# Interpolating two chunks with diagonal matmuls, and moving the opening's sums from VectorE to ScalarE and TensorE

## The chip, the core and the metric

The kernel runs on one core of a Trainium2 chip. The engines are TensorE (PE, with its weight loads PEld), VectorE (DVE), ScalarE (ACT), GpSimd (POOL) and SyncE (SP, which here issues most DMAs). Each engine runs its own instructions in order. Matmuls write PSUM, and results have to be copied from there. The metric is device time of one execution in microseconds; before the change it is 7589.68 us, the median of 3 runs (7587.77 to 7598.68).

## What is computed

Two layers over an image of 4 batches x 128 channels x 64 x 64. The first is a deformable convolution: every output position reads nine taps, each at a fractional position that a small convolution predicts, so each tap is a weighted sum of four neighbours ("corners").

```
def deform_forward(x, w_off, b_off, w_mask, b_mask, weight, bias):
    offset = conv2d(x, w_off, b_off)
    mask = jax.nn.sigmoid(conv2d(x, w_mask, b_mask))
...
    samples = bilinear_sample(x, py, px)
    samples = samples * mask[:, None]
...
    out = jnp.einsum('bckhw,ock->bohw', samples, w_flat)
    return out + bias[None, :, None, None]
```

The second is attention of 16 heads of 8 over the 4096 positions of each batch, with queries, keys and values from the same cosine features, then a small feed-forward layer and a choice of two experts of eight:

```
    qkv = _qz_ring(heads + rx_theta)
    q = jnp.transpose(qkv, (0, 2, 1, 3))
    scores = jnp.einsum('bhsd,bhtd->bhst', q, q) / np.sqrt(D)
    attn = jax.nn.softmax(scores, axis=-1)
    ctx = jnp.einsum('bhst,bhtd->bhsd', attn, q)
```

Everything is float32, and all 4096 keys of a batch are attended to by all its queries.

## The kernel before

**Chunks and units.** A batch is cut into 8 chunks of 512 positions. `prepare` brings a batch through normalization, a table of corners in DRAM, the offsets (`offsets`, which gives the gather indices and the corner weights `wt`), and then `deform`, which walks over units: 12 to a chunk, each of 128 positions and 3 taps. For a unit POOL issues three indirect DMAs (L625) that bring, for each position, four corners of 128 channels into `v`. DVE multiplies `v` with the weights (L645, 1536 elements a partition) and adds twice (L650, L651), which leaves three tap samples with positions on the partitions. The convolution needs channels on the partitions.

**Two ways to turn the samples.** In most chunks DVE transposes blocks (L686), a DMA stores them to `smd`, and `convolved` reads them back as `sT`. In the first two chunks of batch 0 TensorE transposes them (three transposes a unit, L662) into PSUM, and DVE copies the result to `sT_first` (L665) one unit later: the copy waits in the list `moved`. After the last unit of a chunk, `convolved` runs 18 matmul steps (nine taps, two halves; L281 is the helper `by_columns`, which makes each product of four column pieces), DVE adds bias and input (L758), and `features` turns the chunk into keys, queries and values, stored to DRAM with SP and loaded by the attention. `offsets` leaves the indices and weights of the image's second half in `rest`; in batch 0 they are computed after the last unit of chunk 0. Gathers run up to four units ahead in the first three chunks.

**Attention as a list of runs.** A run is one query chunk, one group of four heads and some key tiles of 128. Each step (`scores`, two exponentials on ACT of 128x1024, then `context`) handles one tile; the context of a run adds up in a single PSUM bank, `acc`. Scores are issued up to two steps ahead. Batch 0 starts before all its chunks exist, so its first runs take only the keys at hand: run kinds FIRST, MORE and LAST leave partial sums in DRAM (`partd`). FIRST stores its sum. MORE loads the earlier sum into `cu` at its first step (L1454), DVE adds `acc` (L1488) and the sum is stored again (L1126). Here `opening` counts the first 26 runs: 12 FIRST and 14 MORE, with chunk 0 (16 steps), chunk 1 (48), chunk 2 (40) and chunk 3 (56). Every MORE run among them has four steps.

**Order.** PE, DVE, SP and POOL get their order by hand: the class `Beside` plans, step by step, which pieces of the preparation go between attention steps. A piece announces its cost on PE and DVE with `need(pe=..., dve=..., lat=..., after=...)`; `beside.now`, `beside.dve` and `beside.pool` are the planned times, and `beside.later(when, emit)` issues a DMA when the plan reaches that time. At the end of a run the plan sets DVE's time to at least 1.9 us after the present step and adds the sum. ACT alone is ordered by the scheduler. Until chunk 0 is ready (`alone`) PSUM for the preparation comes from the three score tiles, afterwards from one bank, `ps_m`. The tag `st` has three buffers, `v` three, `cu` two, `acc` one.

Of the kernel before, what the change touches and what calls it, by code (L numbers as in the profile page):

```python
# [9 lines left out]
F32 = mybir.dt.float32  # L10
# [214 lines left out]
def kernel(  # L225
# [373 lines left out]
    def deform(b, tab, idx, wt, rest):  # L599
# [12 lines left out]
        def gather(last):  # L612

            nonlocal issued
            while issued < len(units) and issued <= last + (4 if early(issued) else 2):
# [12 lines left out]
                    )  # L628
                ahead.append((v, beside.gathered()))

        sent = 0.0
        moved = []
        gather(-1)
        for n, (ch, kg, j) in enumerate(units):
            progress[b] = 0.1 + 0.9 * n / len(units)
            if b == 0 and n == 36:
                yield need(dve=5.0)
                settle()
            while not ahead:
                yield need(lat=0.5)  # L640
            v, landed = ahead.pop(0)
            v4 = v.rearrange("p k (q c) -> p (k q) c", c=C)
            w12 = wt[:, j, 3 * kg : 3 * kg + 3, :].rearrange("p k q -> p (k q)")
            yield need(dve=ve(1536), after=landed)
            nc.vector.tensor_tensor(v4, v4, w12[:, :, None].to_broadcast([P, 12, C]), ALU.mult)  # L645
            if moved:
                yield need(pe=0.01, dve=ve(384))
                moved.pop()()
            yield need(dve=ve(768) + ve(384))
            nc.vector.tensor_tensor(v[:, :, : 2 * C], v[:, :, : 2 * C], v[:, :, 2 * C :], ALU.add)  # L650
            nc.vector.tensor_tensor(v[:, :, :C], v[:, :, :C], v[:, :, C : 2 * C], ALU.add)  # L651
            if b == 0 and ch < 2:


                if n % 12 == 0:
                    while len(summed) < ch:
                        yield need(lat=0.5)
                    sT = big.tile([P, KK, CH], F32, tag="xs", name=f"sT_first{ch}")
                yield need(pe=tr(3), lat=FREE, hold=True)
                pt = misc(f"sT_ps{j}_{kg}")  # L660
                for k in range(3):
                    nc.tensor.transpose(pt[:, P * k : P * (k + 1)], v[:, k, :C], ident)  # L662

                def move(sT=sT, kg=kg, i=j % 4, pt=pt):
                    nc.vector.tensor_copy(  # L665
                        sT[:, 3 * kg : 3 * kg + 3, P * i : P * (i + 1)],
                        pt[:, : 3 * P].rearrange("p (k c) -> p k c", c=P),
                    )

                moved.append(move)  # L670
                beside.later(beside.now + 0.8, lambda n=n: gather(n))
                if n % 12 == 11:
                    yield need(pe=0.01, dve=ve(384))
                    moved.pop()()
                    featuring.append(True)
                    beside.add("prepare", convolved(b, ch, sT), 0.5, True)
                    if ch == 0:
                        yield from rest
                continue

            yield need(dve=ve(384))
# [36 lines left out]

    def convolved(b, ch, sT=None):
# [16 lines left out]
        if not in_order:  # L736
# [1 line left out]
            yield need(lat=6.0)  # L738
            get(1)
            yield need(lat=4.0)  # L740
        for k in range(KK):
# [378 lines left out]

        beside.later(beside.dve, put)

    def park_sums(g, sc, cu):
# [6 lines left out]
        beside.later(beside.dve, put)  # L1130

# [139 lines left out]
            es.append(e)  # L1271
        return es

    def context(acc, run, t, es):
        b, g, _, ts, _ = runs[run]
        qf = keys[b, g, t // 4][1]
        flat = qf.rearrange("p t x -> p (t x)")
        width = 32 if t == ts[0] else QW
        for h in range(4):
            first = QG * (t % 4) + QW * h  # L1280
            nc.tensor.matmul(  # L1281
                acc[32 * h : 32 * h + width, :],
                lhsT=flat[:, first : first + width],
                rhs=es[h // 2][:, h % 2, :],
                start=(t == ts[0]), stop=(t == ts[-1]),
            )


    WHOLE, FIRST, MORE, LAST = range(4)
# [118 lines left out]
    with tc.manual_schedule(engines={PE, DVE, SP, POOL}):  # L1408
# [6 lines left out]
        while n < len(steps):  # L1415
# [48 lines left out]
            if following:  # L1464
# [7 lines left out]
                if takes[run + 1] and at == len(ts) - 5:  # L1472
                    fetch_values(run + 1)
                    for giver in takes[run + 1]:
                        for kt in range(4):
                            granted(lambda a=(run + 1, giver, kt): fetch(*a))
            context(acc, run, t, es.pop(0))
            n += 1
            if at == 0 and takes[run]:
                beside.add("turned", from_turned(run, acc), -1)  # L1480
            if at < len(ts) - 1:
                continue
            beside.dve = max(beside.dve, beside.now + 1.9) + ve(512)
            if kind in (WHOLE, FIRST):
                cu = work.tile([P, 512], F32, tag="cu", name=f"cu{run}", bufs=NCU)
                nc.vector.tensor_copy(cu, acc)  # L1486
            else:
                nc.vector.tensor_tensor(cu, cu, acc, ALU.add)  # L1488
            if kind in (WHOLE, LAST):
                park_context(b, g, sc, cu)  # L1490
            else:
                park_sums(g, sc, cu)
        alone.append(True)
        beside.drain()

# [72 lines left out]
```

## Time and profile before

| | |
|---|---|
| median of 3 runs | 7589.68 us |
| the profiled execution | 7632.52 us |
| its span, first to last instruction | 7630.7 us |
| PE busy | 7132.4 us (93%) |
| ACT busy | 6855.1 us (90%) |
| DVE busy | 4479.3 us (59%) |
| POOL busy | 1653.8 us (22%) |
| L645 multiply, 128x1536 | 384 x 1735 ns mean |
| L650, L651 adds, 128x768 and 128x384 | 384 x 956 ns, 384 x 562 ns |
| L1486 copy of `acc`, L1488 add | 128 x 691 ns, 38 x 687 ns |
| L1270 exponential, 128x1024 | 7400, 6852.0 us together |

Times in the timeline are microseconds from the start of the span. In a line of the timeline the first number is the start, the second how long it took, and the brackets at the end give how long the engine had been idle and what ended that. In the views of waits the first number is the total in us, the second how often, the third the longest. "Granted clock" is the share of full speed at which TensorE was clocked.

### The profile page before, as it was taken

What the parts mean: (1) busy time and instruction counts of PE and PEld (TensorE: products, weight loads), DVE (VectorE), ACT (ScalarE), POOL (GpSimd) and SP (SyncE); (2) the same over time, 40 slices, a digit from 0 to 9 for tenths busy, and PEclk for the clock granted to TensorE, in tenths of its full rate; (3) what the DMA queues carried; (4) which work ended last, traced back from release to release, by engine and by line L of the source; (5) the groups of instructions that cost most, each with busy time, mean ns of one, the idle gap of its engine ahead of it and who ended that gap; (6) DMA issues with size and microseconds to landing.
All of it is one profiled execution on the core that took longest, in us unless ns stands there. A gap on an engine that the chain in (4) does not pass through costs nothing.

```text
span 7630.7 us, 180510 instructions
## 1 busy us (share of the span) xinstructions
PE 7132.4 (93%) x73736; PEld 2383.1 (31%) x73736; DVE 4479.3 (59%) x8976; ACT 6855.1 (90%) x7441; POOL 1653.8 (22%) x1326
## 2 busy tenths in 40 slices
PE   3679899899999999999999999989999999999997
PEld 2122232223333333333333323323333333333333
DVE  6766356667444867776554677775444545455534
ACT  0569899899999999999999988989999999999995
POOL 5544034443000432422000334331000000000000
PEclk6889999999999999999999999999999999999998
DMA  6677567978445878887655688897554466667662
GB/s 176 208 212 222 137 209 238 302 235 295 151 172 196 289 231 268 282 273 239 203 179 185 232 274 287 286 309 251 184 175 162 148 232 230 234 217 244 222 204 64
DMA packets 909787, 1689.50 MB, mean 221 GB/s; under 512 B 150754, under 2 KB 384124, under 8 KB 858268
## 3 DMA queue, kind: packets, MB, share of 16 engines
q1 hardware_dynamic: 809102, 1371.37, 54.5%
q0 software_dynamic: 92160, 302.06, 12.5%
q8 instruction: 579, 9.49, 0.5%
q10 hardware_dynamic: 7694, 4.52, 0.2%
q14 instruction: 252, 2.06, 0.1%
HBM read 1027.51 MB, written 650.14 MB: 220 GB/s over the span
## 4 chain that ended last, share of the span: by engine, by line
PE 82%; DMA 8%; DVE 4%; issue 3%; ACT 2%; SPq 1%; POOL 1%; another core or an unknown queue 0%; ACTq 0%; POOLq 0%; DVEq 0%
PE acc L1281 40%; PE sc L1261 24%; PE acc L1214 5%; PE e_ps L281 4%; PE conv_ps L281 4%; DMA et<-etd 3%; PE f_ps L281 2%; ACT e L1270 2%; DMA sT<-smd 1%; PE om_ps L533 1%; DMA etd<-st 1%; DVE v L645 1%; DMA smd<-tr 1%; POOL v L625 0%; PE ao_ps L281 0%
## 5 line engine op out<-in xcount | busy, mean ns | idle before, releaser
L1270 ACT ACTIVATE e<-sc 128x1024 f32<-128x1024 f32 x7400 | 6852.0, 1076 | 637.9 <-PE sc L1261 456.3
L1281 PE MATMUL acc<-e,qf 128*9 128x512 f32 (+1 forms) x29600 | 3946.4, 602 | 33.8 <-DVE cu L1488 15.2
L1261 PE MATMUL sc<-qT,kT 32*128 32x512 f32 x14800 | 2380.9, 500 | 193.8 <-ACT e L1270 97.7
L1261 PEld LDWEIGHTS sc<-qT,kT 32*128 32x128 f32 x14800 | 948.2, 183 | 3663.1 <-ACT e L1270 3140.8
L625 POOL DMA_INDIRECT v<-tab,idx x1152 | 1450.7, 1259 | 1679.6 <-DVE tr L686 1058.0
L1140 DVE STREAM_TRANSPOSE st<-e 128x1024 f32<-128x1024 f32 x792 | 937.3, 1221 | 774.8 <-ACT e L1270 651.0
L1281 PEld LDWEIGHTS acc<-e,qf 128*9 128x9 f32 (+1 forms) x29600 | 682.3, 91 | 629.3 <-issue 345.8
L396 POOL TENSOR_TENSOR r<-ln_t,expo 128x4 f32<-128x4 f32 x96 | 112.2, 1170 | 3111.0 <-DVE ln_t L394 3073.8
L645 DVE TENSOR_TENSOR v<-v,wt 128x1536 f32<-128x1536 f32 x384 | 666.1, 1735 | 102.9 <-DMA v<-tab,idx 88.2
L1214 PE MATMUL acc<-et,qv 128*9 128x128 f32 x12672 | 509.2, 277 | 58.9 <-DMA et<-etd 45.5
L1065 DVE TENSOR_TENSOR eo<-e_ps,gt 128x512 f32<-128x512 f32 x256 | 175.2, 686 | 549.1 <-PE e_ps L281 540.3
L650 DVE TENSOR_TENSOR v<-v 128x768 f32<-128x768 f32 x384 | 367.1, 956 | 9.8
L281 PE MATMUL conv_ps<-sT,wconv_sb 128*32 128x256 f32 x4320 | 352.3, 400 | 11.0 <-DMA sT<-smd 8.8
L1214 PEld LDWEIGHTS acc<-et,qv 128*9 128x9 f32 x12672 | 270.8, 90 | 263.2 <-issue 220.9
L1486 DVE COPY cu<-acc 128x512 f32<-128x512 f32 x128 | 88.5, 691 | 349.0 <-PE acc L1281 290.5
L686 DVE STREAM_TRANSPOSE tr<-v 128x128 f32<-128x128 f32 x1080 | 249.3, 281 | 45.2 <-DMA etd<-st 36.5
L651 DVE TENSOR_TENSOR v<-v 128x384 f32<-128x384 f32 x384 | 215.7, 562 | 13.3
L396 POOL TENSOR_TENSOR rstd<-lt_t,expo 128x4 f32<-128x4 f32 x32 | 59.4, 1856 | 515.2 <-DVE lt_t L394 494.9
L281 PE MATMUL f_ps<-w_sb,h 128*32 128x128 f32 x4096 | 167.6, 282 | 1.5 <-issue 1.5
L950 DVE TENSOR_SCALAR h<-h_ps,b_sb 128x512 f32<-128x512 f32 x128 | 94.9, 744 | 100.3 <-PE h_ps L948 85.0
L823 POOL COPY fx<-rn 128x512 f32<-128x512 f32 x32 | 26.9, 840 | 535.2 <-DVE rn L822 338.2
L965 DVE TENSOR_TENSOR a<-a,f_ps 128x512 f32<-128x512 f32 x32 | 22.0, 686 | 202.9 <-PE f_ps L281 202.5
(224 smaller groups left out, 3148.5 us busy)
## 6 DMA issues: line engine op xcount, KB each, us to landing
etd<-st SPq DMA_DIRECT2D x396, 1024.0 KB
et<-etd SPq DMA_DIRECT2D x396, 1024.0 KB
kT<-kTd SPq DMA_DIRECT2D x372, 256.0 KB
smd<-tr SPq DMA_DIRECT2D x360, 192.0 KB
sT<-smd SPq DMA_DIRECT2D x360, 192.0 KB
qT<-qTd SPq DMA_DIRECT2D x166, 256.0 KB
atd<-cu SPq DMA_DIRECT2D x128, 256.0 KB
qf<-fqd SPq DMA_DIRECT2D x372, 72.0 KB
```

Source lines behind the costliest of these rows:

```text
L281: nc.tensor.matmul(dst[c : c + 32], lhsT=lhsT[:, c : c + 32], rhs=rhs, start=start, stop=stop)
L625: nc.gpsimd.indirect_dma_start(out=v[:, k, :], out_offset=None, in_=tab, in_offset=bass.IndirectOffsetOnAxis(ap=idx[:, j, kk : kk + 1], ax ...
L645: nc.vector.tensor_tensor(v4, v4, w12[:, :, None].to_broadcast([P, 12, C]), ALU.mult)
L650: nc.vector.tensor_tensor(v[:, :, : 2 * C], v[:, :, : 2 * C], v[:, :, 2 * C :], ALU.add)
L651: nc.vector.tensor_tensor(v[:, :, :C], v[:, :, :C], v[:, :, C : 2 * C], ALU.add)
L686: nc.vector.transpose(out=tr9[:, k, :, j % 4, :], in_=v[:, k, :C].rearrange("p (c i) -> p c i", i=32),)
L1065: nc.vector.tensor_tensor(ws[hf], pe.rearrange("p (e c) -> p e c", c=C), gt[:, i, 4 * hf : 4 * (hf + 1), None].to_broadcast([P, 4, C]), AL ...
L1140: nc.vector.transpose(out=st[:, :, 2 * pr : 2 * pr + 2, :].rearrange("p o h (q j) -> p o (h q) j", j=32), in_=es[pr].rearrange("p h (q o i ...
L1214: nc.tensor.matmul(acc[32 * h : 32 * h + QW, P * kt : P * (kt + 1)], lhsT=qv[:, at : at + QW], rhs=e[:, :, h, 32 * t : 32 * (t + 1)], star ...
L1261: nc.tensor.matmul(ps[i // 2][:, i % 2, :], lhsT=kT[h : h + 32, P * (t % 4) : P * (t % 4 + 1)], rhs=qT[h : h + 32, :], start=True, stop=True,)
L1270: nc.scalar.activation(e, ps[pr], AF.Exp, scale=1.0 / math.sqrt(HD))
L1281: nc.tensor.matmul(acc[32 * h : 32 * h + width, :], lhsT=flat[:, first : first + width], rhs=es[h // 2][:, h % 2, :], start=(t == ts[0]), ...
```

## The change

The diff has two parts.

*First two chunks of batch 0.* DVE no longer multiplies the gathered corners. It multiplies the identity matrix by the twelve weights of a unit, which gives twelve diagonal matrices of 128 x 128 in `dg` (a buffer of tag `st`). TensorE multiplies each gathered corner block with its diagonal matrix and adds the four corners of a tap in PSUM: product with the weight, sum and transposition are one chain of matmuls. The two DVE adds and the three transposes go. For chunk 0 the convolution's taps are issued as soon as three of its nine are complete in `sT` (function `taps`), into a PSUM tile `po` that is held through the chunk, and `convolved` then skips them. The second half's weights (`rest`) come after unit 5 instead of after unit 11.

*First 26 runs.* ACT copies `acc` to `cu`. In MORE runs the reloaded sum, `cu`, is added by TensorE before that: the last piece of the run's chain is a product of the identity with `cu`. DVE does nothing for these sums, and the plan reserves no DVE time for them. The store is planned 3.0 us after the present step instead of at DVE's planned time.

```diff
+        def taps(sT, kg):
+            for k in range(3 * kg, 3 * kg + 3):
+                for hf in range(2):
+                    yield need(pe=MM256, lat=FREE, hold=None)
+                    half = slice(256 * hf, 256 * (hf + 1))
+                    by_columns(
+                        po[:, half], wconv_sb[:, k, :], sT[:, k, half],
+                        k == 0 and hf == 0, k == KK - 1 and hf == 1,
+                    )
...
-            yield need(dve=ve(1536), after=landed)
-            nc.vector.tensor_tensor(v4, v4, w12[:, :, None].to_broadcast([P, 12, C]), ALU.mult)
+            first = b == 0 and ch < 2
+            if first:
+                yield need(dve=ve(1536))
+                dg = work.tile([P, 4, 4, P], F32, tag="st", name=f"dg{j}_{kg}", bufs=NST)
+                dg = dg.rearrange("p r h x -> p (r h) x")[:, :12]
+                nc.vector.tensor_tensor(
+                    dg, ident[:, None, :].to_broadcast([P, 12, P]),
+                    w12[:, :, None].to_broadcast([P, 12, P]), ALU.mult,
+                )
+            else:
+                yield need(dve=ve(1536), after=landed)
+                nc.vector.tensor_tensor(v4, v4, w12[:, :, None].to_broadcast([P, 12, C]), ALU.mult)
             if moved:
                 yield need(pe=0.01, dve=ve(384))
                 moved.pop()()
+                if ch == 0 and j % 4 == 0:
+                    yield from taps(sT, kg - 1)
...
                     sT = big.tile([P, KK, CH], F32, tag="xs", name=f"sT_first{ch}")
-                yield need(pe=tr(3), lat=FREE, hold=True)
-                pt = misc(f"sT_ps{j}_{kg}")
+                    if ch == 0:
+                        po = misc("conv_first")
                 for k in range(3):
-                    nc.tensor.transpose(pt[:, P * k : P * (k + 1)], v[:, k, :C], ident)
+                    yield need(pe=4 * MM128, lat=FREE, hold=True, after=landed)
+                    if k == 0:
+                        pt = misc(f"sT_ps{j}_{kg}")
+                    for q in range(4):
+                        by_columns(
+                            pt[:, P * k : P * (k + 1)], v4[:, 4 * k + q], dg[:, 4 * k + q],
+                            q == 0, q == 3,
+                        )
...
+                if n == 5:
+                    yield from rest
                 if n % 12 == 11:
                     yield need(pe=0.01, dve=ve(384))
                     moved.pop()()
+                    if ch == 0:
+                        yield from taps(sT, kg)
                     featuring.append(True)
-                    beside.add("prepare", convolved(b, ch, sT), 0.5, True)
-                    if ch == 0:
-                        yield from rest
+                    beside.add("prepare", convolved(b, ch, sT, po if ch == 0 else None), 0.5, True)
                 continue
...
-    def context(acc, run, t, es):
+    def context(acc, run, t, es, had):
...
-                start=(t == ts[0]), stop=(t == ts[-1]),
+                start=(t == ts[0]), stop=(t == ts[-1] and had is None),
             )
+        if t == ts[-1] and had is not None:
+            by_columns(acc, ident, had, False, True)
...
-            context(acc, run, t, es.pop(0))
+            by_act = run < opening
+            context(acc, run, t, es.pop(0), cu if by_act and kind == MORE else None)
...
-            beside.dve = max(beside.dve, beside.now + 1.9) + ve(512)
+            if not by_act:
+                beside.dve = max(beside.dve, beside.now + 1.9) + ve(512)
             if kind in (WHOLE, FIRST):
                 cu = work.tile([P, 512], F32, tag="cu", name=f"cu{run}", bufs=NCU)
+            if by_act:
+                nc.scalar.copy(cu, acc)
+            elif kind in (WHOLE, FIRST):
                 nc.vector.tensor_copy(cu, acc)
             else:
                 nc.vector.tensor_tensor(cu, cu, acc, ALU.add)
...
-                park_sums(g, sc, cu)
+                park_sums(g, sc, cu, beside.now + 3.0 if by_act else beside.dve)
```

More of the change, by code (lines that the diff above doesn't have):

```diff
@@ L648, in deform @@
                 moved.pop()()
[L649 to L652, printed above, removed]
+                if ch == 0 and j % 4 == 0:
+                    yield from taps(sT, kg - 1)
+            if first:
                 if n % 12 == 0:
@@ L674, in deform @@
                     moved.pop()()
+                    if ch == 0:
+                        yield from taps(sT, kg)
                     featuring.append(True)
-                    beside.add("prepare", convolved(b, ch, sT), 0.5, True)
-                    if ch == 0:
-                        yield from rest
+                    beside.add("prepare", convolved(b, ch, sT, po if ch == 0 else None), 0.5, True)
                 continue
+            yield need(dve=ve(768) + ve(384))
+            nc.vector.tensor_tensor(v[:, :, : 2 * C], v[:, :, : 2 * C], v[:, :, 2 * C :], ALU.add)
+            nc.vector.tensor_tensor(v[:, :, :C], v[:, :, :C], v[:, :, C : 2 * C], ALU.add)
             yield need(dve=ve(384))
@@ L717, in deform, with convolved @@
             yield need(lat=1.0)
-    def convolved(b, ch, sT=None):
+    def convolved(b, ch, sT=None, po=None):
         xr = work.tile([P, CH], F32, tag="p2", name=f"xr{b}_{ch}", bufs=NP2)
@@ L740, in convolved @@
             yield need(lat=4.0)
-        for k in range(KK):
+        if po is not None:
+            yield need(pe=0.01, dve=ve(128, 4), lat=0.2)
+        for k in range(KK) if po is None else ():
             if k == 2 and not in_order:
@@ L1121, in park_context, with park_sums @@
         beside.later(beside.dve, put)
-    def park_sums(g, sc, cu):
+    def park_sums(g, sc, cu, when):
         def put():
@@ L1129, in park_sums @@
         storing.add((g, sc))
-        beside.later(beside.dve, put)
+        beside.later(when, put)
     def turn(es, run, t):
```

## The prediction

> **What bounds the kernel now.** I read the page's slices first, then the busy time by stage, then the ACT timeline (what ended each long idle time), the timeline of the first chunk, and last DVE's waits.
>
> The page, share of busy time in 40 slices of 190.8 us:
>
> ```profile
> PE   3679899899999999999999999989999999999997
> DVE  6766356667444867776554677775444545455534
> ACT  0569899899999999999999988989999999999995
> ```
>
> From the fourth slice on, PE and ACT are full and DVE is not. The attention loop holds that part: 7,400 exponentials, 6852 us of ACT, fixed work. What can be won or lost there is small. The first three slices are not full on anything, so I cut them at the moments where ACT's long waits end:
>
> ```profile
> core 0: us, PE busy (x) PEld busy (x) DVE busy (x) ACT busy (x) POOL busy (x), PEclk, DMA share, GB/s
> 0.00:180.00 180.00, 59.69 (x548) 38.30 (x548) 123.98 (x207) 1.95 (x3) 95.79 (x80) 0.69 0.59 170
> 180.00:272.00 92.00, 47.51 (x360) 16.07 (x358) 67.74 (x120) 30.60 (x32) 55.21 (x40) 0.72 0.61 188
> 272.00:382.00 110.00, 88.11 (x660) 25.06 (x658) 75.59 (x150) 80.49 (x86) 54.13 (x43) 0.86 0.77 233
> 382.00:531.00 149.00, 105.36 (x790) 29.19 (x790) 91.26 (x162) 92.35 (x99) 73.82 (x56) 0.82 0.72 212
> ```
>
> ```profile
> 180.42 5.61 ACT L1270 ACTIVATE e<-sc 128x1024 f32<-128x1024 f32 x6 [125.74 <-PE sc L1261]
> 272.33 5.60 ACT L1270 ACTIVATE e<-sc 128x1024 f32<-128x1024 f32 x6 [37.53 <-PE sc L1261]
> 382.08 1.94 ACT L1270 ACTIVATE e<-sc 128x1024 f32<-128x1024 f32 x2 [10.76 <-PE sc L1261]
> 530.58 5.65 ACT L1270 ACTIVATE e<-sc 128x1024 f32<-128x1024 f32 x6 [9.17 <-PE sc L1261]
> ```
>
> The reader is to see four gates: 180, 272, 382 and 531 us, when chunks 0, 1, 2 and 3 have keys and queries. Up to 531 ACT works 205 us and idles 326. The work between two gates is fixed (16, 48 and 40 steps of about 1.87 us), so a gate that comes earlier is gain only if the last of them, 531, comes earlier. After it ACT idles 49 us up to 960 and is 94% busy for the rest. The time follows the preparation up to gate 3.
>
> How the first chunk is prepared:
>
> ```profile
> 85.89 1.76 DVE L645 TENSOR_TENSOR v<-v,wt 128x1536 f32<-128x1536 f32 x1 [1.36 <-DMA v<-tab,idx]
> 86.30 2.16 POOL L625 DMA_INDIRECT v<-tab,idx  x1 [0.30 <-issue]
> 87.56 0.55 DVE L665 COPY sT_first<-sT_ps 128x384 f32<-128x384 f32 x1
> 111.12 1.76 DVE L645 TENSOR_TENSOR v<-v,wt 128x1536 f32<-128x1536 f32 x1 [1.43 <-DMA v<-tab,idx]
> 131.99 1.13 DVE L758 SCALAR_TENSOR_TENSOR xr<-conv_ps,bconv_sb,xr 128x128 f32<-128x128 f32 x4 [5.52 <-PE sT_ps L662]
> ```
>
> DVE waits for a gather before each multiply, while POOL never pauses more than 0.30 us: the chunk runs at POOL's pace, one unit in 5.05 us (the multiplies at 80.84, 85.89, 91.03). Two gathers of a unit take 0.95 to 1.03 us, the one issued under the multiply 2.0 to 2.3. From the last landing (111.1) to the bias of the convolution (131.99) pass 20.9 us.
>
> DVE's waits in the last stage before gate 3:
>
> ```profile
> DVE cu L1486 <- PE acc L1281: 12.7, 1, 12.7
> DVE cu L1486 <- PE sc L1261: 7.6, 1, 7.6
> DVE cu L1488 <- PE acc L1281: 7.0, 1, 7.0
> ```
>
> DVE stands still with its preparation queued behind a sum that attention has not finished. All such waits in front of cu between 180 and 515 us come to 62.9 us (16.2, 14.5 and 32.2 by stage).
>
> **The change part by part.**
>
> *Interpolation, 24 units.* Gone from DVE: the two adds, 0.96 + 0.56 = 1.52 us a unit. The multiply stays (1.76 us, now of the identity by the weights), as does the copy (0.55). It no longer waits for the landing. PE loses three transposes (0.88 us) and gets 12 products of four column pieces. Nearest row for one: f_ps, same helper, same 128 columns: 167.6 us for 4096 instructions, eight to a product, 0.33 us. Low end by om_ps: 18 taps of 256 columns in 7.89 us, 0.44, half of it 0.22. High end at half clock: conv_ps needs 2.79 us for 24 instructions where it later needs 1.50, so 0.33 x 1.86 = 0.61. A unit thus costs 2.6, 3.9 or 7.3 us. I take 3.9, since the work comes every 1.3 to 2.3 us with the gathers, and wherever the trace shows PE busy in every 5 us stretch (300 to 365) the granted clock is 1.00; it is 0.50 from 55 to 115 with PE 17% busy. At 3.9 it fits into POOL's 5.05.
>
> The Trainium skill (TensorE: Matmul & The Clock Gate, Part 1) has the clock fall after an idle window of about 3.4 us and rise after a busy one. By it the clock would hold at full with 1 us gaps; by the low rows alone chunk 0 would take 12 x 7.3 = 88 us, 27 more.
>
> Does chunk 0 go faster per unit? POOL's bare need is 3 x (0.95 + 0.30) = 3.75 us, and the multiply lengthens one gather by 1.2. It is still there once a unit, with two operands from SBUF as before, so I take 5.05, no gain; the low end is 12 x 1.2 = 14 us gained.
>
> On that lock the Trainium skill (SBUF — State Buffer, Who interferes with whom) says both that a DVE instruction with two SBUF inputs blocks a GpSimd one that reads SBUF, and that tensor_tensor did not hold up descriptor generation. The trace sides with the first (0.95 against 2.16 us). By the second the gain would be the 14 us.
>
> *Tail of chunk 0 and gate 0.* Of 18 taps, 12 are done before the last third. After 111.1: last four products 1.3, copy 0.55, handovers 0.3, six taps at 0.50 (24 instructions, three taps, in 1.50) = 3.0: ready at 116.3. High end, last unit cold: 7.3 + 0.55 + 0.3 + 6 x 0.93 = 124.9. I take 118: 14 us gained (7 to 16). The second half's weights, 6.9 us of DVE (116.3 to 123.1), move to after unit 5, into six units with 5.05 - 2.31 = 2.7 us free: hidden; without that cover they cost their 7 us. The features of chunk 0 (132 to 160 on DVE) have about two units between them: 2 x 1.52 = 3. Gate 0: 17 earlier.
>
> *Chunk 1.* Nine units from 156.85 to 197.7, 4.5 us each; POOL's floor of 3.75 allows 6.8 us, PE's in-order queue with attention may eat all: I take 2. Gate 1: 19 earlier.
>
> *Sums, 26 runs (12 first, 14 more).* DVE loses 26 x 0.69 = 18 us, 18 of the sums (12.4 us) before 515, and the 62.9 us of waits; the hand-written order also no longer reserves 1.9 us plus the sum on DVE at each run's end. Upper end 75. Low end 0: the first 14.1 us wait on the convolution that the next DVE instruction wants too, and after 388 the convolution of chunk 3 is paced by PE, one tap in each step (418 to 457). Chunk 3's own sums (291 to 388) lie behind 14.5 us of waits and five copies, 18 us, and these are on its path. I take 20 of 75. Gate 3: 39 earlier.
>
> ACT gets 26 copies of 128x512. By its 128x144 (0.33 us) and 128x1024 (1.02) rows that is 0.62 each; before gate 3 the 326 idle us hide 18 of them. PE gets 14 additions through the identity, each like a context step: 1.04. Eight runs lie behind gate 3, six with additions: 5 + 6 = 11 us, partly overlapping: I take 8 (0 to 11). ACT's copy waits for the last context, and behind it wait the next exponentials, at most two steps ahead already; the accumulator stays single. A reload that lands late now stops PE, not DVE: see the slower rival. The part store's due time and cu's two buffers remain; its SP issue count is unchanged.
>
> *Sum:* -17 - 2 - 20 + 8 = -31. Profiled span 7630.7 (time 7632.5, 1.8 around it) becomes 7600. The three timed runs have a median of 7589.7, 43 lower all along, so 7589.7 - 31 = 7559.
>
> **The rivals.**
>
> *The head start is lost before gate 3.* For it: between 388 and 531 PE pacing, SP stores (359 to 370, 490 to 497) and landings of 8 to 12 us set the pace. Against it: those move with their inputs. Then gate 3 keeps only the 18 us that lie on chunk 3's own path, less 2 for the queue, and the copies take 8 of them: 7582. Chance 0.18.
>
> *Slower: PE stands at reloaded sums.* Each of the 14 runs issues its reload at its first step and needs it after four, 7.4 us. Two reloads took 8.2 (issued 370.3) and 6.7 us (460.1). Until now DVE waited and PE still issued one step of scores. The price: 14 x (1.87 + 1.04) = 41, with 26 x 0.62 = 16 of copies 57; less gate 0's 17: +40, 7630. It decides once most reloads need more than 7.4 us. Against it: ACT has idle time in most of these runs. Chance 0.15.
>
> *Slower: PE is the bound of both chunks.* At half clock chunk 0 takes 27 more, chunk 1 12 x (7.3 - 4.5) = 34, less 20 for waits and 14 for the tail: +27, 7617. Chance 0.07.
>
> *The copy does not come free of a table.* One ACT_TABLE_LOAD (1.28 us) serves all exponentials; the trace has no copy on ACT. Were each copy to change the table, 52 x 1.28 = 67 us, largely in idle time: 7585. Chance 0.03. The Trainium skill (ScalarE: Activation LUTs, Table sets) says copy is in every set, which makes it 0.
>
> *All of the waits pass through,* 60 of 75: 7519. Chance 0.12.
>
> **How the numbers follow.** The forecast itself has 0.45, with its own range 7535 to 7592 (waits 0 to 40, tail 7 to 16). Over all cases the range is 7520 to 7630. About 0.2% (15 us) is what a measurement tells from no change. Faster: 0.12 + 0.42 of the forecast's 0.45 = 0.54. Same: 0.03 + the lost head start 0.18 + the table's 0.03 less a share = 0.22. Slower: the two rivals and that share, 0.24.
>
> **What would show it.** ACT's first exponential near 163 us and the bias of chunk 0 near 118; gathers still 2.0 to 2.3 us under the multiply; unit pace 5.05; PE clock 1.00 in 60 to 110; third gate near 490; no DVE wait on acc before it; PE waits on the part reload under 20 us. It is wrong if gate 0 comes early and gate 3 does not, or if PE waits for reloads by more than 40 us.

## The result, and the profile after

The changed kernel takes 7646.49 us (median of 5 runs, 7632.09 to 7653.97); the kernel before takes 7587.77 us in the same series (5 runs, 7567.27 to 7598.68). The recorded ratio is 1.0083 (the medians alone give 1.0077), 95% interval 1.0071 to 1.0094: slower by 59 us, where 31 us faster was forecast.

One warning on the two profiles shown: the profiled execution of the kernel before (7632.5 us) was 43 us above the 7589.7 us that the prediction started from, that of the changed kernel (7634.8 us) is 12 us below its median. The two traces therefore look equally long, though the kernels are not. Traces of both kernels from one set of runs follow with the experiments.

The page of the changed kernel, busy tenths in 40 slices and the granted clock:

```profile
PE   6678999999999999999999999989999999999997
DVE  4656446666444777777544677775444545455534
ACT  0468998898999999999999989989999999999995
PEclk8889999999999999999999999999999999999998
```

PE is busy in the first slices now, and DVE is less so. ACT, which has to do the fixed work, starts later: it has lost a tenth in slices 2, 4, 7 and 10 and won one in 5 and 11. The first stage in numbers (columns as in the prediction: busy us of PE, PEld, DVE, ACT, POOL, then the clock, the DMA share and GB/s):

```profile
0.00:180.00 180.00, 107.22 (x2020) 79.25 (x2020) 85.94 (x157) 1.95 (x3) 71.53 (x73) 0.87 0.53 149
```

DVE gave up 38 us there, as it should. POOL gave up 24 us too: the gathers wait now. And the gates of ACT:

```profile
191.92 5.61 ACT L1301 ACTIVATE e<-sc 128x1024 f32<-128x1024 f32 x6 [137.01 <-PE sc L1292]
300.18 5.61 ACT L1301 ACTIVATE e<-sc 128x1024 f32<-128x1024 f32 x6 [47.24 <-PE sc L1292]
549.99 5.64 ACT L1301 ACTIVATE e<-sc 128x1024 f32<-128x1024 f32 x6 [36.60 <-PE sc L1292]
```

Gate 0 is at 192 instead of 180 and gate 1 at 300 instead of 272. For gate 3 the first exponential on chunk 3's keys has to be compared: it is number 209, since chunks 0 to 2 have 16 + 48 + 40 steps of two exponentials. It stands at 549.99 here and in the trace of before at

```profile
513.08 5.60 ACT L1270 ACTIVATE e<-sc 128x1024 f32<-128x1024 f32 x6 [27.35 <-issue]
```

so gate 3 is 37 us late. The row at 531 that the prediction took for it is number 217, a second, shorter wait. From here on "gate 3" is number 209. All gates were forecast to come earlier.

What the first chunk waits for, in the timeline of the changed kernel:

```profile
56.32 3.76 PE L281 MATMUL sT_ps<-dg,v 128*32 128x128 f32 x63 [2.41 <-DVE dg L660]
...
63.29 0.42 PE L281 MATMUL sT_ps<-dg,v 128*32 128x128 f32 x4 [1.01 <-issue]
...
69.01 0.95 POOL L625 DMA_INDIRECT v<-tab,idx  x1 [0.30 <-issue]
69.69 1.12 PE L281 MATMUL sT_ps<-dg,v 128*32 128x128 f32 x4 [1.46 <-issue]
...
72.02 0.56 DVE L690 COPY sT_first<-sT_ps 128x384 f32<-128x384 f32 x1 [14.14 <-remote]
72.26 0.95 POOL L625 DMA_INDIRECT v<-tab,idx  x1 [2.30 <-remote]
```

The first unit's products begin at 56.3 with 63 matmuls in 3.8 us, then come in groups of one to six, most of them four, with breaks of 0.3 to 1.5 us in which PE waits for nothing that the profile shows, and the copy can start only at 72.0. From 59.0 POOL issues a gather every 1.25 us, without a gap; PE is fast again when this burst has ended (the 2.30 us of idle POOL). After that a unit takes 5.1 us (copies at 72.0, 77.1, 82.2 and 87.3), and now POOL and DVE wait for PE. The bias of chunk 0 comes at 139.58 us, not at 118.

### The profile page after: what moved, and what is told of

Its sections match the earlier page's. It is cut to its first block, busy times and chain, and to the rows that moved or that the text cites. A ratio compares the mean times of both kernels' runs of the same rounds, so it can differ in the third digit from the quotient of the medians.

```text
span 7632.9 us, 185148 instructions
## 1 busy us (share of the span) xinstructions
PE 7186.2 (94%) x76080; PEld 2439.8 (32%) x76080; DVE 4431.4 (58%) x8902; ACT 6864.0 (90%) x7467; POOL 1648.5 (22%) x1326
## 4 chain that ended last, share of the span: by engine, by line
PE 83%; DMA 7%; DVE 4%; issue 2%; ACT 2%; SPq 1%; another core or an unknown queue 0%; ACTq 0%; POOL 0%; POOLq 0%; DVEq 0%
PE acc L1312 40%; PE sc L1292 24%; PE acc L1245 5%; PE conv_ps L281 4%; PE e_ps L281 4%; DMA et<-etd 2%; PE f_ps L281 2%; ACT e L1301 2%; DMA sT<-smd 1%; PE sT_ps L281 1%; PE om_ps L533 1%; DMA etd<-st 1%; DVE v L666 1%; DVE st L1171 0%; PE ao_ps L281 0%
## 5 line engine op out<-in xcount | busy, mean ns | idle before, releaser
L666 DVE TENSOR_TENSOR v<-v,wt 128x1536 f32<-128x1536 f32 x360 | 625.1, 1736 | 112.6 <-DMA v<-tab,idx 97.6
L708 DVE TENSOR_TENSOR v<-v 128x768 f32<-128x768 f32 x360 | 343.9, 955 | 9.9
L281 PEld LDWEIGHTS conv_ps<-sT,wconv_sb 128*32 128x32 f32 x4320 | 88.1, 109 | 177.2 <-issue 167.7
```

The source lines that it names most:

```text
L281: nc.tensor.matmul(dst[c : c + 32], lhsT=lhsT[:, c : c + 32], rhs=rhs, start=start, stop=stop)
```

## The experiments

There were five sets, each on one chip with its own runs of the kernel before. These had medians of 7579.1, 7583.8, 7463.0, 7606.6 and 7607.8 us, so only ratios are compared between sets. Set 1 is e1 to e4, set 2 e5 to e8, set 3 e9 to e12, set 4 e13 to e16, set 5 the last two.

**Each part alone (set 1).** e1_before is the kernel before. e2_interp_only is the changed kernel with

```diff
-            by_act = run < opening
+            by_act = False
```

and e3_sums_only is the kernel before with the second part of the change alone.

> The kernel before, unchanged, for a trace on the same chip as the runs beside it. All theories: a ratio of 1.000 (0.996 to 1.004); the first exponential near 180 us, the gate of chunk 3 (ACT's restart after its longest idle time before 560 us) near 531 us. Its span tells whether the 7630.7 us of the first profiled execution are typical beside a median of 7588.

> The interpolation part alone; the sums stay on VectorE. Theory 1 (TensorE's 96 pieces a unit pace the first two chunks, and the gates come late): this alone carries most of the loss, ratio 1.005 to 1.010, first exponential at 188 to 195 us, bias of chunk 0 near 140 us. Theory 2 (TensorE stands at the reloaded sums): ratio 0.997 to 1.002, first exponential late all the same, but caught up by 531 us. Theory 3 (the planner's order happens to fall badly, in no one place): anything, and no match with the part's own gates.

> The sums part alone; the chunks are interpolated on VectorE as before. Theory 1: ratio 0.996 to 1.001, first exponential at 180 us as before, gate of chunk 3 not later than 531 us. Theory 2: ratio 1.004 to 1.009, TensorE's waits for the reload (acc<-cu) 25 us or more before 560 us and the gate of chunk 3 at 545 us or later.

| run | median us | ratio to before | 95% interval |
|---|---|---|---|
| e1_before (one execution) | 7580.17 | | |
| e2_interp_only | 7601.76 | 1.0031 | 1.0021 to 1.0041 |
| e3_sums_only | 7573.79 | 0.9995 | 0.9985 to 1.0005 |
| both, e5_after (set 2) | 7637.39 | 1.0073 | 1.0049 to 1.0097 |
| both, e16_after (set 4) | 7671.92 | 1.0079 | 1.0062 to 1.0095 |

The interpolation loses 0.3%, less than the first theory had expected of it, the sums change nothing that can be told, and together they lose 0.75%. So the parts do not add. e1's execution lies 1 us from the median of its set (7579.1 us).

**Fewer pieces (e4, set 1).** Each product as one matmul instead of four column pieces:

```diff
-                        by_columns(
-                            pt[:, P * k : P * (k + 1)], v4[:, 4 * k + q], dg[:, 4 * k + q],
-                            q == 0, q == 3,
+                        nc.tensor.matmul(
+                            pt[:, P * k : P * (k + 1)], lhsT=v4[:, 4 * k + q], rhs=dg[:, 4 * k + q],
+                            start=q == 0, stop=q == 3,
                         )
```

> The whole change, but each product with a diagonal matrix is one matmul over all 128 columns instead of four pieces of 32: a quarter of the instructions for the same products. Theory 1 in the form that instructions are short, not clock: a unit's products take under 3.5 us instead of 4.9, bias of chunk 0 at 115 to 128 us, first exponential at 165 to 180 us, time 0.2 to 0.6% below the changed kernel's. If the array's time is what is short instead: a unit takes as long or longer, and the time is the changed kernel's or above. Theory 2: no change of the time beyond 0.1%.

7620.64 us, 1.0050 (1.0033 to 1.0067). Chunk 0's units are not held up: the first copy comes at 60.3 us, against 69.5 in e2 of the same set, and the last at 111.6. With a quarter of the instructions and the same gathers the hold-up of the first unit is gone. And yet the bias comes at 129.53, as in e1 (129.6). The timeline of e4 shows what holds it:

```profile
111.49 3.08 PE L281 MATMUL conv_first<-sT_first,wconv_sb 128*32 128x256 f32 x48
112.09 0.94 POOL L625 DMA_INDIRECT v<-tab,idx  x1 [0.30 <-issue]
...
125.85 0.94 POOL L625 DMA_INDIRECT v<-tab,idx  x1 [0.30 <-issue]
129.53 1.13 DVE L789 SCALAR_TENSOR_TENSOR xr<-conv_first,bconv_sb,xr 128x128 f32<-128x128 f32 x4 [17.38 <-remote]
```

PE's last taps are recorded as started by 114.2, close to the forecast. But DVE is released only at 129.5, 2.7 us after the last of twelve gathers in a row, for chunk 1, has ended.

**The changed kernel again, gathers less far ahead, reloads earlier, chunk 0 alone (set 2).**

> The changed kernel unchanged, on the chip of the other experiments: ratio to the kernel before 1.008, some 7640 us. It gives the size of what one part alone (1.0031) and the other alone (0.9995) leave unexplained: about 0.5%, 38 us. In its trace the gates are expected near 192, 300 and 550 us again.

```diff
-            while issued < len(units) and issued <= last + (4 if early(issued) else 2):
+            while issued < len(units) and issued <= last + 2:
```

> The changed kernel, gathers of the first three chunks at most two units ahead instead of four. Theory A (POOL's uninterrupted gathers hold PE up: the first unit's products took from 56 to 72 us, until the first burst of gathers ended): unit 0's copy comes by 64 instead of 72 us, gate 0 by 182 instead of 192, the time 10 to 25 us below the changed kernel's. Theory B (the column pieces alone are too many for PE, whatever POOL does): PE still needs about 5 us a unit, gate 0 stays at 190 or later, the time is the same or longer, since the gathers come later.

e7 asks for the reloaded sum of the next run in the second step of a run, with three buffers for `cu`:

```diff
                 if at == 1:
+                    if run + 1 < opening and following[4] == MORE:
+                        reload(run + 1)
```

> The changed kernel, each reloaded sum of the first 26 runs asked for in the second step of the run before instead of in its own first step, with a third buffer for cu. Theory C (PE stands at the reloads, 48.6 us of waits): these waits fall below 15 us and the time falls by 15 to 30 us. Theory D (the waits only show work that was late anyway, and the stores and loads of the preparation in SP's queue set the gates): the waits go and the time stays within 8 us.

e8 is e2 with the interpolation on PE for chunk 0 only, and chunk 1 on DVE as before:

```diff
-            first = b == 0 and ch < 2
+            first = b == 0 and ch < 1
```

> The interpolation part alone, and of it chunk 0 alone: chunk 1 is interpolated as in the kernel before, the sums too. With both chunks it was 7601.8 us, +0.31%. If chunk 0 makes the loss (the first unit held up by the gathers), 7600 stays. If chunk 1 makes it (its products stand in PE's queue between attention steps), the time returns to 7580 or below. Gate 0 is 192 in either case, gate 1 300 or 285.

e6: 7630.42 us, 1.0061 (1.0043 to 1.0078). Its first copy came at 68.0 us and the second at 79.3; in e5 of the same set they came at 66.8 and 79.6. The gap between them stayed, gate 0 stayed at 195, and nothing was decided between A and B. The time of e6 is 7 us below that of e5 although its gate 3 is 6.7 us later (550.6 against 543.9).

e7: 7635.45 us, 1.0070 (1.0052 to 1.0089), against 7637.39 of the same set. The waits on reloads are gone, and nothing is gained. PE's waits between 560 and 680 us, in us in total, times, longest; first e5, then e7:

```profile
PE acc L281 <- DMA cu<-part: 10.7, 2, 7.8
PE sc L1292 <- DMA qT<-qTd: 3.3, 2, 2.5
```

```profile
PE sc L1292 <- DMA qT<-qTd: 12.7, 3, 8.6
```

PE now stands for nearly the same time (12.7 us, against 14.0) at the queries, which come next in SP's queue. So the theory that the waits on reloads cost the time (C) falls. The 48.6 us in its expectation counts PE's weight loads too, which stand beside the matmuls; the matmuls alone wait 22.5 us in four waits.

e8: 7591.24 us, 1.0014 (1.0004 to 1.0025). Beside e2's 1.0031 in set 1, chunk 0 makes about half of the interpolation's loss and chunk 1 the other half; the intervals leave the shares wide open.

**What holds PE, and attention's loads on another queue (set 3).** In e9 SP loads plain rows for chunk 0 in place of the gathers, so chunk 0's samples are not the reference's:

```diff
+                    if b == 0 and n < 12:
+                        at = 256 * (3 * n + k) % 4096
+                        nc.sync.dma_start(
+                            out=v[:, k, :],
+                            in_=tab[at : at + 256].rearrange("(p r) c -> p (r c)", r=2),
+                        )
+                        continue
```

In e10 and e12 POOL has to read the bias result before the gathers of chunk 1:

```diff
+            nc.gpsimd.tensor_copy(seen, xr[:, CH - 1 : CH])
+            biased.append(True)
```

e10 is e4 with this; e12 is the kernel before with this, the early taps and the second half's weights after unit 5. In e11, the changed kernel, ACT issues the loads of `kT` and `qf` for the first four chunks, and of `qT` and `cu` in the first 26 runs:

```diff
-                    nc.sync.dma_start(out=cu, in_=partd[g][sc])
+                    (nc.scalar if run < opening else nc.sync).dma_start(out=cu, in_=partd[g][sc])
```

> The changed kernel, with the gathers of chunk 0 left out: SP loads as many bytes in the same row length, but consecutive rows of the table, so chunk 0's samples are not at the predicted positions. Theory A (POOL's own work on uninterrupted gathers holds PE up): unit 0's copy comes by 64 instead of 72 us, a unit takes under 4.5 us, the bias of chunk 0 comes by 122 instead of 140. Theory B (the column pieces are too many for PE, whatever POOL does): units stay at 5 us and the bias at 136 or later. Theory E (the traffic into SBUF holds PE up, whoever starts it): PE stays at 4 to 10 matmuls a us wherever some 60 packets a us arrive, as with gathers.

> The kernel with whole-width products (both parts), and POOL has to read the bias result of chunk 0 before it starts the gathers of chunk 1. Before, the last tap was recorded at 114.2 us, PE's semaphore came at 129.5, right after twelve gathers in a row had ended. Theories A and E: the bias comes at 115 to 119 instead of 129.5, gate 0 at 167 to 172 instead of 181.7; the time falls by 5 to 12 us below 7620.6 if the lead lasts, by nothing if the later gathers of chunk 1 take it. If something else holds the semaphore, the bias stays at 127 or later.

> The changed kernel, with attention's own loads in the first 26 runs (reloaded sums, queries, keys and values of chunks 0 to 3) issued by ACT instead of SP. Theory D (they stand behind the preparation's stores and loads in SP's queue, and PE waits for whichever comes last): PE's waits on reloads and queries between 560 and 680 us, 14 us, fall below 4, gate 3 comes by 536 instead of 544, the time falls by 10 to 25 us below 7637. If the lateness has another cause (the stores these loads follow), the waits and the time stay within 6 us; if ACT stands at the loads' own waits, the time rises.

> The kernel before (DVE interpolates, sums on DVE) with three side edits of the change alone: early taps of chunk 0, the second half's weights after unit 5, and the hold of chunk 1's gathers until the bias of chunk 0. If bursts of gathers are what delays the end of chunk 0, the bias comes at 116 to 120 instead of 129.6 and gate 0 at 166 instead of 178. The time is 7565 to 7576 if gate 3 follows by half of it, 7580 if the lead is lost.

| run | us | ratio (interval) | bias of chunk 0 | gate 0 |
|---|---|---|---|---|
| e9_plain_loads | 7485.95 (one execution) | | 111.5 | 165.6 |
| e10_hold | 7505.97 | 1.0046 (1.0029 to 1.0064) | 114.1 | 173.2 |
| e11_act_queue | 7497.19 | 1.0046 (1.0029 to 1.0063) | 119.8 | 174.7 |
| e12_taps_hold | 7460.20 | 1.0002 (0.9993 to 1.0012) | 120.4 | 179.6 |

In this set PE was not held up. e11 leaves chunk 0 exactly as the change has it, and its copies and its bias are

```profile
60.89 0.56 DVE L690 COPY sT_first<-sT_ps 128x384 f32<-128x384 f32 x1 [3.01 <-PE sT_ps L281]
63.64 0.56 DVE L690 COPY sT_first<-sT_ps 128x384 f32<-128x384 f32 x1 [0.52 <-PE sT_ps L281]
...
119.78 1.12 DVE L789 SCALAR_TENSOR_TENSOR xr<-conv_first,bconv_sb,xr 128x128 f32<-128x128 f32 x4 [2.94 <-PE conv_first L281]
```

60.9 instead of 72.0, and 119.8 instead of 139.6, with the same instructions under the same gathers. e9 could therefore not isolate the gathers: it missed its aim, and the early biases of e10 and e12 cannot be put down to the hold either. The hold shows what is late next. POOL of e12:

```profile
121.62 0.18 POOL L809 COPY seen<-xr 128x1 f32<-128x1 f32 x1 [12.78 <-DVE xr L803]
122.31 0.97 POOL L630 DMA_INDIRECT v<-tab,idx  x1 [0.51 <-PE x_ps L816]
...
139.02 2.21 POOL L630 DMA_INDIRECT v<-tab,idx  x1 [0.30 <-issue]
141.25 1.40 POOL L396 TENSOR_TENSOR rstd<-lt_t,expo 128x4 f32<-128x4 f32 x1
```

The features' `rstd` is computed on POOL; its input was there at 124.7, and it stood 16.6 us behind twelve gathers. Before the change it was at 136.9 (e1, set 1), so the whole lead is gone.

**Both kernels side by side, the queue again (set 4).** e13 is e11's kernel once more, e14 the sums part alone with the same loads on ACT's queue.

> The kernel before, profiled beside the changed kernel of the same set. If this set is like the third (7463 us), the bias of chunk 0 comes near 125 and gate 0 near 175; if it is like the first two, 130 and 178.

> The changed kernel. If the hold-up of PE under the gathers is the larger share of the loss, then where it is absent (bias of chunk 0 before 125 us) the ratio is 1.003 or less; if it is present (bias at 140), 1.007 again. If SP's queue is the larger share, the ratio is 1.005 or more in either case.

> The changed kernel with attention's loads of the first 26 runs issued by ACT instead of SP. If SP's queue makes the loss that neither part makes alone (about 0.4%, 30 us), this kernel is 12 to 30 us faster than the changed kernel of the same set, and the stretch from the 256th to the 384th exponential shrinks from 147 to about 137 us. If not, both are within 6 us.

> The sums part alone (0.9995 before), with the same loads issued by ACT. In its trace gate 3 came 8.5 us earlier, and the stretch from the 256th to the 384th exponential took 147 instead of 130 us, with PE waiting 11.2 us for reloads. If SP's queue is the cause, that stretch shrinks to 135 or less and the ratio falls to 0.997 to 0.999. If not, 0.9995 stays.

PE was held up here (bias 144.4) and the ratio of e16 was 1.0079. e13: 7666.0 us, 1.0078 (1.0061 to 1.0095); the stretch from the 256th to the 384th exponential shrank from 155.8 to 146.3 us, but the time by 6 us at most, inside the spread. e14: 7618.08 us, 1.0017 (1.0006 to 1.0028): worse than the 0.9995 without the move, its gate 1 at 283 instead of 270 in e15 (ACT itself stood at a key load). Theory D is not borne out by the time.

e11 and e13 are the same kernel, without and with the hold-up of PE: 1.0046 and 1.0078. Across these two sets, then, the hold-up goes with some 0.3% of loss, and more than that is lost without it.

**The order at gate 3, and a version from what held (set 5).** In every trace so far with both parts, except e6, PE stands just before gate 3 at taps of chunk 4, and SP, where it loads the keys, loads chunk 4's samples ahead of chunk 3's keys. SP and then PE of e16:

```profile
531.87 6.73 SPq L760 DMA_DIRECT2D sT<-smd  x8
539.68 0.34 SPq L1270 DMA_DIRECT2D kT<-kTd  x1
```

```profile
545.48 2.79 PE L281 MATMUL conv_ps<-sT,wconv_sb 128*32 128x256 f32 x24 [28.20 <-DMA sT<-smd]
552.91 0.80 PE L1292 MATMUL sc<-qT,kT 32*128 32x512 f32 x4 [4.64 <-DMA kT<-kTd]
```

With one part or none, and SP's queue unchanged, PE stands at the keys themselves. e18 puts the order right:

```diff
+        while b == 0 and ch == 4 and (0, 0, 3) not in keys:
+            yield need(lat=0.5)
```

> The changed kernel, with the convolution of chunk 4 held in the plan until the keys of chunk 3 have been asked for; the order is otherwise the planner's. If the flipped order is the part that neither edit loses alone, gate 3 comes 54 to 57 us after the bias of chunk 3 instead of 69, and the time falls by 10 to 20 us: ratio 1.0055 to 1.0065 instead of 1.0073 to 1.0083. If the delay at gate 3 is made good later anyway, gate 3 moves and the ratio stays at 1.007 or above. What remains then stands in the first two chunks, where PE's queue has become the one that all wait for.

e17b is e12 with the sums part, the order of e18, and the gathers of chunk 1 let go only once the features' `rstd` is issued:

```diff
-            by_act = False
+            by_act = run < opening
...
+            def release():
+                biased.append(True)
```

> A version from what held: the interpolation of the kernel before, the early taps of chunk 0, the second half's weights after unit 5, the gathers of chunk 1 issued only after chunk 0's rstd (in an earlier run they had delayed it by 17 us on POOL), the sums by ACT and PE, and the order guard at gate 3. Bias of chunk 0 at 120 and rstd at 125 instead of 137: gate 0 at 164 to 168 instead of 178, gate 3 15 us earlier, ratio 0.997 to 0.999. If chunk 1's later gathers take the lead back, gate 1 is at 268 or later and the ratio 0.9995 to 1.001.

SP and then PE of e18:

```profile
528.24 0.76 SPq L1272 DMA_DIRECT2D kT<-kTd  x1
...
531.90 7.69 SPq L762 DMA_DIRECT2D sT<-smd  x8
```

```profile
534.41 1.22 PE L1294 MATMUL sc<-qT,kT 32*128 32x512 f32 x6 [19.10 <-DMA kT<-kTd]
```

Gate 3 comes at 535.3 instead of 553.8, and the time is 7672.79 us, 1.0087 (1.0071 to 1.0104): no gain at all from 18.5 us at gate 3. e17b brought gate 0 to 164.5 (180.8 in e15) and ended at 7633.43 us, 1.0037 (1.0026 to 1.0048). No version that was run beats the kernel before; e3 and e12 equal it.

**Which gate counts.** The next table is read off the timelines of DVE (bias of a chunk, the DVE line that ends its convolution) and ACT (the exponential that ends a gate; gate 3 is exponential 209, the last gate is exponential 585), in us:

| | bias 0 | bias 1 | bias 3 | gate 3 | bias 7 | last gate | ACT idle there |
|---|---|---|---|---|---|---|---|
| e1_before | 129.6 | 218.9 | 447.7 | 502.3 | 844.4 | 903.2 | 22.4 |
| e2_interp_only | 142.5 | 249.9 | 471.6 | 526.7 | 867.8 | 926.3 | 22.1 |
| e3_sums_only | 128.9 | 207.3 | 439.4 | 493.8 | 844.8 | 901.8 | 11.2 |
| e15_before | 132.2 | 221.6 | 452.0 | 509.1 | 851.8 | 910.5 | 22.4 |
| e16_after | 144.4 | 255.6 | 485.2 | 553.8 | 897.8 | 957.3 | 8.5 |
| e18_keys_first | 140.8 | 253.6 | 483.8 | 535.3 | 896.2 | 955.4 | 11.9 |
| e17b_taps_sums | 120.0 | 223.7 | 450.4 | 502.8 | 870.2 | 927.2 | 9.7 |

The last gate belongs to chunk 7, 57 to 60 us after its bias, in every row. The trace of before shows it too:

```profile
917.79 5.60 ACT L1270 ACTIVATE e<-sc 128x1024 f32<-128x1024 f32 x6 [21.77 <-PE sc L1261]
```

ACT waits 22 us there, so a lead at gate 3 can be spent waiting at this one. In e18 most of it was gone before: against e16 it was 18.5 us at gate 3, 9.5 at the 256th exponential and 1.9 at the last gate, where ACT waited 3.4 us more. The time goes more nearly with the chain of convolutions, bias 0 to bias 7. Against the kernel before of the same set, bias 7 is late by 23.4 us in e2, by 0.4 in e3 and by 46.0 in e16; the medians differ by 22.7, -5.3 and 65.3 us. No run moved bias 7 alone, and e6 speaks against taking it for the whole: its bias 7 came 15.4 us later than that of e5 (903.3 against 887.9), and its profiled execution was 6.5 us shorter (7631.6 against 7638.1).

## Why the prediction was wrong

- **The step that failed first: "The time follows the preparation up to gate 3."** e18 shows that it does not: 18.5 us at gate 3, nothing in the time. A later wait, of 21.77 us at 917.79, stood in the trace of before; the prediction passed it over as part of "after it ACT idles 49 us up to 960". All of the 39 us earlier at gate 3 was summed up for a gate that does not set the end. What sets it instead is known in part: bias 7 fits e2 and e3, 46 of the 65 us of e16, and not e6.
- **Interpolation, "I take 3.9" us a unit on PE, pace 5.05 unchanged.** The 17 us gained at gate 0 became 11.5 lost (191.92 against 180.42). Where PE was not held up a unit cost 2.6 us, the prediction's low end and not its 3.9 (e11: so far apart are the copies of units whose samples are there), and the bias was at 119.8, close to the forecast 118. In the series that counts the first unit took 16 us, the later ones 5.1 paced by PE, and the bias came at 139.6. The prediction priced PE by the cost of its instructions and its clock alone, though the trace of before held the hold-up already, in the taps of chunk 0 under the gathers of chunk 1 (us, PE busy, matmuls, clock, DMA share, GB/s):

```profile
118.00:119.00 1.00, 1.00 (x28) 1.00 0.63 164
122.00:123.00 1.00, 0.41 (x2) 1.00 0.64 168
```

  The clock (the feared rival) was not the cause: from 60 to 64 us it was 1.00 in the changed kernel, and PE did 23 matmuls; in e11 it was 1.00 too, and PE did 128. The Trainium skill (TensorE: Matmul & The Clock Gate, Part 1) has the clock fall after an idle window of about 3.4 us. By that it would have stayed at full, but from 68 to 72 us it was 0.50, with no break of PE above 1.46 us from 60 on; the measurement decides.
- **"Ready at 118 ... gate 0: 17 earlier."** Even with the bias at 119.8 (e11) gate 0 was at 174.7, 55 us after it, against 47 in e1. Between the two stood as many multiplies as in e1 (8) and less work of DVE (36.2 against 48.6 us), but 25 gathers instead of 17 in POOL's queue; the 3 us for two units had the wrong sign. The hold in e12 and e17b shows POOL's part: with `rstd` behind the gathers gate 0 is at 179.6 (e12), with `rstd` ahead of them at 164.5 (e17b); these are two sets, with the bias at 120.4 and 120.0.
- **"Chunk 1: I take 2."** From bias 0 to bias 1 took 89 us in e1, 107 in e2 and 96 in e8, where DVE interpolates chunk 1. The low end, "PE's in-order queue with attention may eat all", was named, but not bounded as a loss: chunk 1's products stand between attention steps. In the changed kernel DVE's copies wait 36.9 us for them between 180 and 272.
- **"I take 20 of 75" for the sums.** Alone they moved bias 3 by 8 us, and gave it back before bias 7: from bias 4 to the first tap of chunk 5 pass 63.7, 62.4 and 60.9 us in e1, e2 and e15, but 72.7 in e3, 82.1 in e16 and 72.3 in e18. The samples for these taps were asked for 44 to 54 us after bias 4 in all of them, and the first tap came 13 us after that in the first three, 25 to 28 in the others; in between PE waited for a reloaded sum (5.8 us in e3, 6.1 in e16) or for queries (8.0 in e18). The 62.9 us of waits also held 9.9 us of waits for reloaded sums, which the change hands to PE. With the interpolation on PE the sums brought bias 3 9 us later instead of 8 earlier (33 us late in e16, 24 in e2). The reading is that PE, not DVE, was then what the preparation waited for, so that time given back to DVE was worth nothing; no run isolates this.
- **The rival "PE stands at reloaded sums", 7630.** PE's matmuls stood 22.5 us in four waits, a little above the 20 up to which the prediction held it off, and below the 40 that it named as its sign. It was not the cause: e7 took the waits away and the time did not move, since the next load in the queue was as late.
- **The 8 us after gate 3.** Sizes right: ACT's copy took 0.62 us in the mean, as forecast, the addition 1.04 us in most runs, 1.94 after a wait of 4.9 us or more. No run measures the sum of 8. No table was loaded for the copy (one load in the whole trace, as before), as the Trainium skill (ScalarE: Activation LUTs, Table sets) says.
- **The gather under the multiply, "2.0 to 2.3".** It took 1.55 us, because it starts 1.0 us into the multiply instead of 0.4. It ends 0.81 us after the multiply in both kernels (88.46 against 87.65 before, 75.06 against 74.25 after). So the hold by a two-operand multiply is confirmed, against the sentence in the Trainium skill (SBUF — State Buffer, Who interferes with whom) that tensor_tensor did not hold up descriptor generation.

Left open: why the two parts together delay bias 7 by 46 us, when alone they delay it by 23.4 and 0.4 (the order at gate 3, the reloads and SP's queue were each tried and are not it alone); what holds PE up under the gathers; and some 15 to 20 us more that the changed kernel loses between the 640th and the 1800th exponential (e16 against e15: 48 us late at the one, 67.5 at the other, 64 at the end), for which nothing was tried. e6 does not lose them: that stretch took 1156.5 us there and 1172.5 in e5.

## What to carry to other kernels

Before costing an edit, find the last wait in the trace that its lead would meet: an early gate can be worth nothing while a later one still has idle time in front of it. Price new work from rows that ran beside the same transfers, and not by the clock alone. Moving work to an engine that is 17% busy is only free if that engine's queue is not shared, in order, with work that waits. When a stall is removed, list what comes next in the same queue, because that is often as late.

## What was not expected of the hardware

While POOL issued gathers without a pause (one every 1.25 us), PE got slow, with breaks of 0.3 to 1.5 us between small groups of matmuls, or was done late: 16 us for a first unit that took 4.6 in e11 (changed kernel, 56 to 72 us), 15 us from the last recorded tap to the release of DVE (e4). It ended 2.8 us after the last gather of the burst began in the changed kernel (69.01, PE fast at 71.79), and 3.7 us after it in e4 (125.85, release at 129.53). It seems to need many small matmuls too: with a quarter of them, in e4, chunk 0's units passed under the same gathers without it. The kernel before has it as well, with 2 matmuls a us from 122 to 124 us at a clock of 1.00.

In set 3 the same code ran without it (unit 0 done at 60.9 us), and there the kernel before also took 1.5% less time than in set 1. The traffic as such does not explain it (199 GB/s and 23 matmuls in the changed kernel from 60 to 64 us, 191 GB/s and 92 matmuls in e11 from 72 to 76), nor does the clock. The loading of instructions shows nothing either: its queue moved a packet at 57.6 us and the next at 73.7, after PE had become fast. The cause was not found. In e4 a matmul's recorded start and the release of its result were 15 us apart.
